# One image's top-k attention and the next stage's state scan: the attention cut into pieces and issued between the scan's steps

## The chip, the cores and the metric

The kernel runs on one core of one Trainium2 chip. The metric is device time in microseconds for one launch, all eight images included. Four compute engines work side by side, each on its own queue and strictly in the order of that queue: TensorE (PE, matmuls, with its weight loads listed as PEld), VectorE (DVE), ScalarE (ACT) and GpSimd (POOL). SyncE (SP) issues the DMAs, in order as well. An instruction whose inputs are not ready holds up everything behind it on its engine. SBUF is the large on-chip memory; PSUM is the small one that TensorE writes, in eight banks of 512 float32 per partition.

## The reference

Input `x` is 8 images of 256 channels by 48 x 48 positions, so 2304 tokens of 256 channels each. Two residual layers follow one another, all in float32.

```python
x = x + _L0_conv_ref(_gn(x), W, bias)        # layer 0: top-16 attention
x = x + _L1_conv_ref(_gn(x), ...)            # layer 1: two Mamba blocks

# layer 0, per image
feat, pos = split(tokens @ W.T + bias)       # 256 channels each
pos = pos / max(norm(pos), 1e-12)
sim = pos @ pos.T                            # 2304 x 2304
topksim, topkid = top_k(sim, 16)
out = softmax(topksim) @ feat[topkid]

# layer 1, per image, twice (DEPTH = 2)
xi, z = split(layernorm(x) @ in_w.T)         # 512 channels each
xc = silu(causal_conv4(xi))
dt, B, C = ... from xc                       # dt: 512, B and C: 16 states
h[t] = h[t-1] * exp(dt[t] * A) + dt[t] * B[t] * xc[t]     # 512 x 16 states
y[t] = sum over states of h[t] * C[t]
x = ((y + xc * D) * silu(z)) @ out_w.T
```

`_gn` is a group normalisation over groups of 8 channels and all positions of an image, so each layer needs the whole image before it starts. The recurrence over the tokens has to run in the order of the tokens.

## The kernel before

The images follow one another. For each, `load_x` (L64) loads the image, `layer0` (L181) computes the attention, and `layer1` (L303) the two Mamba blocks. Each of the two opens its own pools for SBUF and PSUM and closes them at its end (L670 to L675).

`layer0` normalises, projects in six chunks of 384 tokens, and then works through 18 tiles of 128 query tokens (L254). For a tile, PE computes 128 x 2304 similarities in five PSUM pieces, which ACT copies out (L246, L250). DVE finds the 16 largest in four passes over the 2304 columns, two `max` and two `match_replace` (L261 to L264), which mark what was taken; ACT takes the exponential (L268) and DVE masks it (L269). PE transposes the masked row blocks (L275), ACT copies them out (L278), PE multiplies them with the features (L283), and the result is scaled, transposed back and added to the image in SBUF (L285 to L290). The similarities of tile t+1 stand ahead of tile t's selection, and four PSUM buffers for each of two kinds allow that. A scheduler orders this layer.

`layer1` is ordered by hand (`manual_schedule`). Its unit of work is one chunk of 384 tokens at one depth: 12 units per image (`order`, L495). A unit has 16 steps (`STEPS`) of 32 channels; a step holds 32 channels x 4 state groups on 128 partitions, with 4 states (`Q`) in the free dimension, and is done in two parts (`PARTS`) of two states. So a unit is 32 parts and an image 384. The loop over parts `m` (L645) issues for each part, in this order: `carry` (ACT copies the last state column, L565), `decay` of the next part (two ACT exponentials into a PSUM tile `da`, L532), `run_scan` (two DVE scans, L550), and then at even parts POOL's work (`pool_part`, L580; `make_bx` two steps ahead, L518) and DVE's `gate` (L605), at odd parts `sum_states` (PE adds the states up, L595) and `out_proj` (L616).

The scan's result has to be multiplied by C. Which engine does it is set by `on_pool` (L510): in 3 of every 8 parts the scan writes `g` in SBUF and POOL multiplies (L580); in the other 5 the scan writes over `da` in PSUM and DVE multiplies (L556). `g` has four buffers (`LAG` + 2), so the scan of step n needs the state sums of step n-4 done.

What the next unit needs (layer norm, input projection, convolution, B, C, dt and the gates z) is computed by the generator `before` (L341 on) in thirteen pieces, one per part, during the current unit (L665). Its `step_size` part applies softplus and sends `dt` and `dt*x` to HBM through two SBUF buffers each (L469, L473); `load_rep` (L317) reads them back spread over the partitions. PSUM in layer 1: two `da` tiles of two banks, three `mm` banks, one bank `y`.

## Time and profile before

| | |
|---|---|
| median of 3 runs | 14379.09 us (14372.37 to 14391.17) |
| the profiled execution | 14374.63 us |
| its span on the core | 14372.7 us |
| busy, DVE | 10997.1 us (77%) |
| busy, PE | 9414.7 us (66%) |
| busy, POOL | 7832.2 us (54%) |
| busy, ACT | 6977.4 us (49%) |
| first scan instruction of the first image | at 501.7 us |
| first scan instruction of the last image | at 13061.8 us |

Seven images lie between the last two rows, so an image takes 1794.3 us, and the last image's layer 1 takes 1310.9 us to the end. The page's second part shows the busy share of each engine in 40 slices of the span; one image is five of them. The page's fifth part groups instructions by line, engine and shape, with busy time, mean duration, and the idle time before them. The trace can be asked for any stretch of time: the busy time of each engine there, who waited for whom, or the instructions in order. PE durations are modelled; the distance from start to start is the firmer number.

### The profile page before, as it was taken

The page shows a single profiled execution, that of the slowest core. Times are in us where ns is not written, and L with a number is a line of the kernel's source. Part 1 is how long each engine was busy: PE and PEld are TensorE (multiplying, and loading weights), DVE is VectorE, ACT ScalarE, POOL GpSimd, SP SyncE. Part 2 cuts the span into 40 slices and gives each one's busy share as a digit, 9 for nine tenths or more (in the row PEclk, how much of TensorE's full clock was granted, in tenths as well). Part 3 has the DMA queues.
Part 4 walks back from the last instruction along what each step waited for, and adds up shares of the span by engine and source line. Part 5 has one row for each costly group of instructions (what it writes and reads, how often), then busy time and mean ns, then how long its engine had stood idle before and what let it go on. Part 6 is the DMA issues. An engine that isn't in the chain of part 4 may idle for free.

```text
span 14372.7 us, 111023 instructions
## 1 busy us (share of the span) xinstructions
PE 9414.7 (66%) x34144; PEld 4778.3 (33%) x34144; DVE 10997.1 (77%) x12021; ACT 6977.4 (49%) x12922; POOL 7832.2 (54%) x4060
## 2 busy tenths in 40 slices
PE   8656596555965559655596555966559655596655
PEld 6322263222632226322263222632226322263222
DVE  6688866888668886688866888668886688866888
ACT  3455534555345553455534555345543455434554
POOL 0477704777047770477705777057770577705777
PEclk9777797777977779777797777977779777797777
DMA  0233302333023330233302333033330333302333
GB/s 19 67 90 85 88 3 67 88 88 87 3 70 87 87 85 3 70 88 87 84 3 71 87 87 84 3 71 87 87 84 3 72 86 88 84 3 71 86 89 79
DMA packets 634854, 960.01 MB, mean 67 GB/s; under 512 B 88560, under 2 KB 608880, under 8 KB 634256
## 3 DMA queue, kind: packets, MB, share of 16 engines
q1 hardware_dynamic: 621312, 948.75, 27.9%
q8 instruction: 269, 4.41, 0.1%
q10 hardware_dynamic: 12944, 4.16, 0.1%
q14 instruction: 329, 2.70, 0.1%
HBM read 778.01 MB, written 174.59 MB: 66 GB/s over the span
## 4 chain that ended last, share of the span: by engine, by line
DVE 36%; PE 31%; ACT 16%; DMA 9%; issue 4%; SPq 2%; POOL 2%; DVEq 0%; ACTq 0%; POOLq 0%
DVE da L550 18%; ACT da L532 9%; DVE g L556 8%; PE po L283 7%; PE psim L246 7%; DVE g L550 4%; DMA dt_d<-dt 4%; DVE xc L409 4%; PE px L436 3%; PE pe L335 2%; PE pt L275 2%; DMA BC<-bc_d 2%; PE y L595 2%; DMA dtxr<-dtx_d 2%; PE pw L616 1%
## 5 line engine op out<-in xcount | busy, mean ns | idle before, releaser
L518 POOL TENSOR_TENSOR bx<-BC,dtxr 128x1536 f32<-128x1536 f32 x1536 | 5270.5, 3437 | 613.2 <-DVE da L550 531.7
L532 ACT ACTIVATE da<-dtr,A_sb 128x384 f32<-128x384 f32 x6144 | 3578.0, 584 | 1389.7 <-DVE g L550 711.1
L550 DVE TENSOR_TENSOR_SCAN da<-da,h_st,bx 128x384 f32<-128x384 f32 x3200 | 3255.6, 1017 | 1174.8 <-ACT da L532 759.7
L595 PE MATMUL y<-g,sel 128*32 128x384 f32 x12288 | 2651.0, 596 | 572.9 <-DVE g L556 542.0
L580 POOL TENSOR_TENSOR g<-g,BC 128x768 f32<-128x768 f32 x1152 | 2083.1, 1808 | 312.8 <-DVE g L550 231.1
L556 DVE TENSOR_TENSOR g<-da,BC 128x768 f32<-128x768 f32 x1920 | 1838.9, 958 | 141.9 <-DVE da L550 2.8
L382 POOL MEMSET vn<- 128x6 f32 x16 | 1.7, 106 | 3416.1 <-PE pr L288 3416.1
L550 DVE TENSOR_TENSOR_SCAN g<-da,h_st,bx 128x384 f32<-128x384 f32 x1920 | 1839.8, 1000 | 0.0
L335 PE MATMUL pe<-vn,in_sb 128*128 128x384 f32 (+1 forms) x3072 | 1251.8, 550 | 536.6 <-ACT z L488 299.2
L595 PEld LDWEIGHTS y<-g,sel 128*32 128x32 f32 x12288 | 743.9, 130 | 2463.8 <-issue 1595.5
L565 ACT COPY h_st<-da 128x2 f32<-128x2 f32 x1600 | 256.4, 160 | 2233.0 <-DVE g L556 2229.9
L589 PE MATMUL y<-xc,dmat 128*128 128x384 f32 x768 | 452.6, 681 | 1295.4 <-DVE yz L605 1295.4
L616 PE MATMUL pw<-yz,ow_sb 128*128 128x384 f32 x1536 | 732.3, 635 | 845.0 <-DVE yz L605 845.0
L246 PE MATMUL psim<-pos 128*128 128x512 f32 (+1 forms) x2880 | 1155.2, 550 | 0.0
L283 PE MATMUL po<-feat,aT 128*128 128x256 f32 x5184 | 1143.9, 379 | 0.0
L436 PE MATMUL px<-xc,xp_sb 128*48 128x384 f32 x768 | 458.8, 771 | 869.3 <-ACT xc L430 869.3
L283 PEld LDWEIGHTS po<-feat,aT 128*128 128x128 f32 x5184 | 974.3, 190 | 128.2 <-ACT aT L278 1.7
L550 DVE TENSOR_TENSOR_SCAN da<-da,bx 128x384 f32<-128x384 f32 x640 | 613.1, 958 | 520.1 <-ACT da L532 261.8
L335 PEld LDWEIGHTS pe<-vn,in_sb 128*128 128x128 f32 x3072 | 594.3, 206 | 1185.1 <-ACT z L488 357.8
L474 POOL TENSOR_TENSOR dtx<-dt,xc 128x384 f32<-128x384 f32 x384 | 374.6, 994 | 970.5 <-ACT dt L470 969.8
L579 POOL COPY h_st<-g 128x2 f32<-128x2 f32 x960 | 180.1, 188 | 1212.8 <-DVE g L550 1205.3
L409 DVE SCALAR_TENSOR_TENSOR xc<-pe,cw,xc 128x384 f32<-128x384 f32 x1152 | 705.8, 614 | 88.0 <-ACT xc L402 48.0
(124 smaller groups left out, 10595.4 us busy)
## 6 DMA issues: line engine op xcount, KB each, us to landing
dtr<-dt_d SPq DMA_DIRECT2D x1536, 192.0 KB, 3.7
dtxr<-dtx_d SPq DMA_DIRECT2D x1536, 192.0 KB, 5.5
BC<-bc_d SPq DMA_DIRECT2D x768, 192.0 KB, 4.8
dt_d<-dt SPq DMA_DIRECT2D x384, 192.0 KB, 4.3
dtx_d<-dtx SPq DMA_DIRECT2D x384, 192.0 KB, 4.2
x<-in_x_dram SPq DMA_DIRECT2D x48, 384.0 KB, 3.8
out_dram<-x SPq DMA_DIRECT2D x96, 192.0 KB, 1.9
bc_d<-dbl SPq DMA_DIRECT2D x96, 48.0 KB, 1.5
```

Of the source, the lines that this page charges most:

```text
L246: nc.tensor.matmul(pm, pos[:, k, t * P : (t + 1) * P], pos[:, k, c0 : c0 + w], start=(k == 0), stop=(k == CB - 1),)
L283: nc.tensor.matmul(po, aT[:, m, :], feat[:, m, :], start=(m == 0), stop=(m == NB - 1))
L335: nc.tensor.matmul(pe, in_sb[:, d, k, e * P : (e + 1) * P], unit["vn"][:, k, lo:], start=(k == 0), stop=(k == CB - 1),)
L409: nc.vector.scalar_tensor_tensor(xc[e], unit["pe"][e][:, k : k + T], cw[:, d, e, k : k + 1], xc[e], ALU.mult, ALU.add,)
L436: nc.tensor.matmul(px[0:E, :], xp_sb[:, d, k, :], xc[k], start=(k == 0), stop=(k == DB - 1))
L518: nc.gpsimd.tensor_tensor(bx, unit["BC"][0], unit["dtxr"][k][:, i % J : i % J + 1, :].to_broadcast([P, Q, T]), ALU.mult,)
L532: nc.scalar.activation(da[:, q], unit["dtr"][k][:, i % J, :], AF.Exp, scale=A_sb[:, unit["d"], i, s : s + 1],)
L550: nc.vector.tensor_tensor_scan(h[:, q], da[:, q], unit["bx"][i][:, s], 0.0 if unit["c"] == 0 else h_st[:, unit["d"], i, s : s + 1], ALU.mu ...
L556: nc.vector.tensor_tensor(g, h, unit["BC"][1][:, p * HQ : (p + 1) * HQ], ALU.mult)
L580: nc.gpsimd.tensor_tensor(g, g, unit["BC"][1][:, qs], ALU.mult)
L595: nc.tensor.matmul(unit["y"][k][o : o + G, :], sel, unit["g"][ii][:, q], start=False, stop=True, skip_group_check=True,)
L616: nc.tensor.matmul(pw, ow_sb[:, unit["d"], k, cb * P : (cb + 1) * P], unit["ys"][k], start=(k == 0), stop=(k == DB - 1),)
```

## The change

All images become one pipeline. `layer0` is now a generator that is stopped after each piece, and the loop over the parts of the scan takes one piece of the next image's attention per part (`next(other, None)`). Only the first image's attention runs by itself, by draining the same generator. The parts of all images form one list of units, so the preparation (`before`) of an image's first unit runs inside the last unit of the image ahead.

For a tile of 128 queries the generator stops 16 times: five pieces for the selection (two `max`, two `match_replace`, and the mask, with the end of the previous tile's work in the first three), then eleven for the transposes, the products with the features and the next tile's similarities. The first selection piece of a tile always falls on part 15 or 31 of a unit. The whole attention of an image takes 339 of the 384 parts: 47 ahead of the first tile (statistics, projections, first similarities), 284 for the tiles, 8 to close.

To make room: the attention has one PSUM bank `mm0` and one `po`, the scan's side one bank `mm` (three before) beside `da` and `y`; the image is not kept in SBUF but read twice from HBM for layer 0 and once more for its residual, and the result of layer 0 goes to HBM (`x1`) and comes back chunk by chunk; the input and output projection weights are loaded once per unit; `bx` has two buffers (three before) and is made one step ahead (two before); dt and dt*x come back in pieces of two steps (four before); the similarities have one buffer.

Other edits: `on_pool` gives POOL 5 of 8 parts for all images but the last, and where both parts of a step are POOL's it multiplies them in one instruction; `dt` has four buffers; the gates z are computed in a generator of their own (`gates`, from part 7 of the same unit on, its silu at part 11); `before` starts at part 11; square root and reciprocal become exponential of a logarithm on ACT and a Newton step of three small DVE instructions; the image's normalisation moves from DVE to ACT; the second normalisation's statistics are taken in 18 x 2 pieces of 128 columns.

```diff
-    xpool = ctx.enter_context(tc.tile_pool(name="xpool", bufs=NCH))
+    keep = ctx.enter_context(tc.tile_pool(name="keep", bufs=2))
+    ps = ctx.enter_context(tc.tile_pool(name="ps", bufs=2, space=PSUM))
+    ctx.enter_context(tc.manual_schedule())
+    def mm(w, name):
+        return ps.tile([P, 512], F32, tag="mm", name=name, bufs=1)[:, :w]
+    def mm0(w, name):
+        return ps.tile([P, 512], F32, tag="mm0", name=name, bufs=1)[:, :w]
...
+    def rsqrt_end(r, var, eps, name):
+        t = small.tile(list(r.shape), F32, tag="newton", name=f"nt_{name}")
+        nc.vector.scalar_tensor_tensor(t, r, -0.5, r, ALU.mult, ALU.mult)
+        nc.vector.scalar_tensor_tensor(t, var, eps, t, ALU.add, ALU.mult)
+        nc.vector.scalar_tensor_tensor(r, t, 1.5, r, ALU.add, ALU.mult)
...
         def similarity(t):
-            s = rows.tile([P, N], F32, tag="sim", name=f"sim_{b}_{t}")
+            s = keep.tile([P, N], F32, tag="sim", name=f"sim_{b}_{t}", bufs=1)
+            pm = None
             for c0 in range(0, N, SW):
                 w = min(SW, N - c0)
-                pm = psum(w, "mm", f"psim_{b}_{t}_{c0}")
+                if pm is not None:
+                    nc.scalar.copy(s[:, c0 - SW : c0], pm)
+                pm = mm0(w, f"psim_{b}_{t}_{c0}")
...
-                nc.scalar.copy(s[:, c0 : c0 + w], pm)
-            return s
+                yield s
+            nc.scalar.copy(s[:, c0:], pm)
+            yield s
+
+        def attend(t, r):
+            po = ps.tile([P, 512], F32, tag="po", name=f"po_{b}_{t}", bufs=1)[:, :C]
+            pt, aT = None, None
+            for m0 in range(0, NB + 8, 4):
+                if aT is not None:
...
+                        nc.tensor.matmul(
+                            po, aT[1][:, m - aT[0], :], feat[:, m, :],
+                            start=(m == 0), stop=(m == NB - 1),
+                        )
...
+                    nc.scalar.copy(
+                        aT[1][:, 0:n, :], pt[1].rearrange("p (m q) -> p m q", q=P)
+                    )
...
+                        nc.tensor.transpose(
...
+                yield po
...
+            nc.vector.max(top[:, 0:8], s)
+            next(done, None)
+            yield
+            nc.vector.match_replace(r, top[:, 0:8], s, TAKEN)
+            next(done, None)
+            yield
+            nc.vector.max(top[:, 8:16], r)
+            next(done, None)
+            yield
...
+            nc.scalar.activation(s, s, AF.Exp)
+            nc.vector.match_replace(r, top[:, 8:16], r, TAKEN)
+            yield
+            nc.scalar.activation(top, top, AF.Exp, accum_out=den)
+            nc.vector.reciprocal(den, den)
+            nc.vector.scalar_tensor_tensor(r, r, TAKEN, s, ALU.is_equal, ALU.mult)
+            yield
+            ahead = similarity(t + 1) if t + 1 < NB else iter(())
+            for i, po in enumerate(attend(t, r)):
+                if i * 4 >= NB:
+                    s = next(ahead, None)
+                yield
+            for s in ahead:
+                yield
+            done = finish(t, po, den)
...
-                dt = tmp.tile([P, T], F32, tag="dt", name=f"dt_{u}_{k}", bufs=2)
+            dt = keep.tile([P, T], F32, tag="dt", name=f"dt_{u}_{k}", bufs=4)
             nc.scalar.activation(dt, pds[k], AF.Softplus, bias=dtb[:, d, k : k + 1])
-                if k == 0:
-                    step_size(3)
+            if k + 1 < DB:
+                step_size(k + 1)
...
+    def gates(unit):
+        u = unit["u"]
+        in_proj(unit, DB)
+        yield
+        for e in range(DB):
+            z = keep.tile([P, T], F32, tag="z", name=f"z_{u}_{e}", bufs=4)
+            nc.scalar.copy(z, unit["pe"][DB + e])
+            unit["z"].append(z)
+            if e + 1 < DB:
+                in_proj(unit, DB + e + 1)
+                yield
+        nc.scalar.preload_act_table_set("silu_and_others")
+        for e in range(DB):
+            nc.scalar.activation(unit["z"][e], unit["z"][e], AF.Silu)
+        nc.scalar.preload_act_table_set("natural_log_exp_and_others")
...
-        def on_pool(i, p):
-            return p == PARTS - 1 and i % J < J - 1
+    def on_pool(unit, i, p):
+        if unit["b"] + 1 < B:
+            return p == PARTS - 1 or i % J == 0
+        return p == PARTS - 1 and i % J < J - 1
...
-            bx = keep.tile([P, Q, T], F32, tag="bx", name=f"bx_{b}_{n}", bufs=3)
+        bx = keep.tile([P, Q, T], F32, tag="bx", name=f"bx_{n}")
...
+    for _ in layer0(0, lefts[0]):
+        pass
+    load_v(units[0])
+    for _ in before(units[0]):
+        pass
...
+    for m in range(PARTS * (NSTEP + LAG + 4)):
...
+        if m % (HOOKS * len(order)) == 0:
+            image = m // (HOOKS * len(order)) + 1
+            other = layer0(image, lefts[image]) if image < B else iter(())
+        carry(m - 1)
+        decay(m + 1)
+        run_scan(m)
+        if p == 0:
+            make_bx(n + 1)
+            pool_part(n - 1)
+            gate(n - LAG - 1)
+            load_out(n - LAG)
+        else:
+            sum_states(n - LAG)
...
+        next(leaving, None)
+        if unit is not None:
...
+            if m % HOOKS == PARTS * (LAG + 1) + 1:
+                behind = gates(unit)
+            next(behind, None)
+            if follow is not None and m % HOOKS == FRONT:
...
+                load_v(follow)
+                front = before(follow)
+            next(front, None)
+        next(other, None)
-    for b in range(B):
-        xs = load_x(b)
-        with ExitStack() as stack:
-            layer0(b, xs, stack)
-        with ExitStack() as stack:
-            layer1(b, xs, stack)
```

More of the change, by code (lines that the diff above doesn't have):

```diff
@@ new lines, in tile_conv_preact, with at @@
+    order = [
+        (i - d, d) for i in range(NCH + DEPTH - 1) for d in range(DEPTH) if 0 <= i - d < NCH
+    ]
+    lefts = [{} for _ in range(B)]
+    units = [
+        dict(b=b, c=c, d=d, u=f"{b}_{c}_{d}", left=lefts[b], pe={}, xc=[], BC=[], z=[], pw=[],
+             dt_d=[], dtx_d=[], dtr={}, dtxr={}, bx={}, g={}, da={}, y={})
+        for b in range(B) for c, d in order
+    ]
+    following = {(un["b"], un["c"], un["d"]): un for un in units}
+    NSTEP = len(units) * STEPS
+    def at(n):
+        return units[n // STEPS], n % STEPS, n % STEPS // J
@@ new lines, in carry, with pool_part @@
+    def carry(m):
+        n, p = divmod(m, PARTS)
+        if not 0 <= n < NSTEP:
+            return
+        unit, i, k = at(n)
+        if unit["c"] + 1 < NCH and not on_pool(unit, i, p):
+            nc.scalar.copy(
+                h_st[:, unit["d"], i, p * HQ : (p + 1) * HQ], unit["da"][i, p][:, :, T - 1]
+            )
+    def pool_part(n):
+        if not 0 <= n < NSTEP:
+            return
+        unit, i, k = at(n)
+        lo = [p for p in range(PARTS) if on_pool(unit, i, p)]
+        if not lo:
+            return
+        qs = slice(lo[0] * HQ, (lo[-1] + 1) * HQ)
+        g = unit["g"][i][:, qs]
+        if unit["c"] + 1 < NCH:
+            nc.gpsimd.tensor_copy(h_st[:, unit["d"], i, qs], g[:, :, T - 1])
+        nc.gpsimd.tensor_tensor(g, g, unit["BC"][1][:, qs], ALU.mult)
```

774 lines of the change are left out of this document (369 added, 405 removed).

## The prediction

> **What bounds the kernel now.** First the page's slices: an image is five of them, and its first has a lower DVE share, an idle POOL and PE at nine tenths of its clock; the other four are the scan.
>
> ```profile
> DVE  6688866888668886688866888668886688866888
> POOL 0477704777047770477705777057770577705777
> ...
> PEclk9777797777977779777797777977779777797777
> ```
>
> Next the busy times (PE, PEld, DVE, ACT, POOL, then granted clock, DMA share, GB/s) in three stretches of the second image: attention, the head of layer 1 before the first scan, the scan.
>
> ```profile
> 1828.00:2243.00 415.00, 387.59 (x1604) 279.04 (x1604) 274.34 (x250) 152.15 (x265) 0.10 (x1) 0.94 0.00 1
> 2243.00:2297.00 54.00, 30.44 (x72) 15.47 (x72) 9.46 (x16) 25.74 (x38) 7.01 (x5) 0.69 0.44 108
> 2297.00:3620.00 1323.00, 763.06 (x2592) 304.27 (x2592) 1089.25 (x1233) 694.26 (x1313) 971.81 (x501) 0.75 0.36 86
> ```
>
> Three bounds in turn: in the attention PE (388 of 415 us) with POOL idle (0.10), in the head a chain, in the scan DVE (1089 of 1323). Attention's DVE work, 274, is what might move under the scan. Who stopped DVE in the scan stretch, and what held ACT (us, times, longest):
>
> ```profile
> DVE da L550 <- ACT da L532: 123.2, 26, 13.1
> DVE da L550 <- issue: 47.8, 6, 12.1
> DVE da L550 <- POOL bx L518: 29.5, 1, 29.5
> ```
>
> ```profile
> ACT dt L470 <- DMA dt_d<-dt: 94.5, 21, 9.8
> ```
>
> Over 200 of the 234 idle us are waits for da, bx or issue; behind them stands ACT, held 94.5 us by the store of dt from its two buffers. Last, the instructions in order, in a steady piece of scan and in one attention tile, and POOL's and ACT's groups:
>
> ```profile
> 2714.35 2.08 DVE L550 TENSOR_TENSOR_SCAN da<-da,h_st,bx 128x384 f32<-128x384 f32 x2
> ...
> 2716.46 0.96 DVE L556 TENSOR_TENSOR g<-da,BC 128x768 f32<-128x768 f32 x1
> ...
> 2717.33 2.08 DVE L550 TENSOR_TENSOR_SCAN da<-da,h_st,bx 128x384 f32<-128x384 f32 x2
> ...
> 2720.39 1.92 DVE L550 TENSOR_TENSOR_SCAN g<-da,h_st,bx 128x384 f32<-128x384 f32 x2
> ...
> 2722.22 2.06 DVE L550 TENSOR_TENSOR_SCAN da<-da,h_st,bx 128x384 f32<-128x384 f32 x2
> ```
>
> ```profile
> 2066.71 2.13 PE L275 MATMUL pt<-ident,left 128*128 128x128 f32 x18
> ...
> 2067.31 2.56 DVE L261 MAX8 top<-sim 128x8 f32<-128x2304 f32 x1 [4.02 <-ACT sim L250]
> ...
> 2068.67 7.94 PE L283 MATMUL po<-feat,aT 128*128 128x256 f32 x36
> ...
> 2078.23 2.54 DVE L269 SCALAR_TENSOR_TENSOR left<-left,sim 128x2304 f32<-128x2304 f32 x1
> ...
> 2078.50 6.18 PE L246 MATMUL psim<-pos 128*128 128x512 f32 x16
> ...
> 2085.12 2.56 DVE L261 MAX8 top<-sim 128x8 f32<-128x2304 f32 x1 [3.42 <-ACT sim L250]
> ```
>
> ```profile
> L518 POOL TENSOR_TENSOR bx<-BC,dtxr 128x1536 f32<-128x1536 f32 x1536 | 5270.5, 3437 | 613.2 <-DVE da L550 531.7
> L532 ACT ACTIVATE da<-dtr,A_sb 128x384 f32<-128x384 f32 x6144 | 3578.0, 584 | 1389.7 <-DVE g L550 711.1
> ...
> L580 POOL TENSOR_TENSOR g<-g,BC 128x768 f32<-128x768 f32 x1152 | 2083.1, 1808 | 312.8 <-DVE g L550 231.1
> ```
>
> A part multiplied by DVE costs it 2.98 us (2714.35 to 2717.33), one left to POOL 1.83 (2720.39 to 2722.22). A tile goes from max to max in 17.81 us; PE's 18 transposes take 2.13, 36 products 7.94, the similarities 1.77 per 512 columns (three and a half such pieces in 6.18), 8.0 in all: 18.5 with 0.44 of closing transposes. Each of DVE's five passes takes 2.54 to 2.56.
>
> **The cut of the time.** Before: 501.7 to the first scan, 7 x 1794.3, 1310.9 for the last image, 14372.7. After, the same cut: E + 7P + Z. The profiled execution is 14374.63, 1.9 over its span; the median lies 4.5 above it.
>
> **E, the exposed first attention.** Statistics end near 32 as now (constants). Projection: a chunk takes 11.6 now (six in 76 us) with four PSUM buffers; with one bank each matmul group waits for the copy ahead; adding up one chunk's matmuls, copies and small steps in series gives 15, six 90. First similarities 11. A tile: DVE's own 14.7 (2 x 2.59 + 2 x 2.66 + 2.7 for mask and reciprocal, 1.5 closing); then PE's 18.2 and, since one bank serves transposes and similarities, about 3.5 of copies left uncovered: 36.5 against 17.8. Eighteen are 657, closing 10: 800. Head 54 now, 62 with one mm bank: **E = 862**, 360 later than now.
>
> **Z, the last image.** Parts stay 5:3, 20.4 us per 8, with 0.46 of gate 20.9: 83.4 per unit; convolutions (12 of 0.61) and norms add 9.8. The dt wait (94.5/12 = 7.9 per unit) goes with four buffers. Late next: ACT at part 11, where the gates' silu with two table loads (1.28 each) stands ahead of the next unit's norm, whose result DVE's next instruction waits for (about 7), and the softplus block, four times 0.58 with a matmul between each and two table loads, about 8.5 against 4.8 of DVE parts in hand (7 with silu). 12 x 107 = **1290** with the tail.
>
> **P, one merged image.** A unit's 32 parts are 20 of POOL's (1.83) and 12 of DVE's (2.98). Per unit DVE has 74 for parts and gates, 9.8 as above, two tiles at 14.7: 113, plus small steps 115. POOL has 16 bx of 3.44, the multiplies at 1.81 and 3.44 with state copies of 0.19, 4 dtx of 1: 98, so moving two parts in eight there costs nothing while DVE's passes cover it. They do in the selection pieces alone. So four stretches:
>
> - Parts 31 to 3, selection: DVE 4 x 1.83 + 2.98 + 14.7 = 25; all else is shorter. Take 26.
> - Parts 4 to 14, transposes, products, similarities, plus output projection, gates z and the next norm: PE 18.5 + 5.3 + 5.3 (16 records each; a 512-column record takes 0.44, so 0.33 for 384) + 5.9 (32 records of state sums at 0.16, pairs in different columns, and the D term) + 4.1 (the norm's three groups, 6.1 in the head at clock 0.69) = 39. DVE has 30, POOL 32. The output projection, first in PE's queue, needs the last gate (3.5). With one bank each, an ACT copy waits for PE and the next matmul for that copy; the state sums stand behind these matmuls, and until they are done `g` is not free and the scan of part 8 waits. At part 11 ACT's z copy, silu with tables and the norm's scaling (0.5 + 4.3 + 1.3, say 6) stand ahead of the mean that DVE waits for, with the scans of parts 12 on behind it. 3.5 + 39 + 6 = 48.5; DVE idles 18.
> - Parts 15 to 19, selection with convolutions: 25 + 7.7 = 33; take 33.5.
> - Parts 20 to 30, with silu, x_proj, softplus: POOL 32 + 4 = 36, PE 30 (18.5 + 5.3 + 5.9), DVE 27; the softplus block holds ACT, and with it the decays and scans, 6 beyond that: 42.
>
> 150 per unit. The 284 tile parts are 8.9 units: 1331. The 47 parts ahead: 11 at POOL's 3.0, 21 with projections at 4.2 (DVE 71, ACT stalls 17), 15 at 4.1 with PE ahead: 183. Eight closing parts at 3.6: 29. The 44 without attention, POOL-bound at 2.95 plus ACT stalls: 152. **P = 1695**, 99 under now.
>
> Costed at nothing: the extra DMA (x three times more, x1 out and back, weights per unit, 33 MB on 120 per image), hidden under a DMA share of 0.36; wholly uncovered it would be 330 us per image at 100 GB/s. SP issues 64 pieces of dt and dt*x per unit (32 before) and some 30 others, at 0.45 about 42 us of 141. C's load waits for a buffer until the unit's last bx, parts 23 to 29, with the queue behind it; the attention's own transfers fall on parts 15 to 17 and 31 to 1, clear of it. Also bx with two buffers: made 3.44 after its part begins, needed two parts later.
>
> **Unknowns.** PE's clock: 0.94 in attention, 0.75 in the scan; I take the former, because PE works almost without gaps in the long stretch. At 0.75 PE's 39 becomes 49: 164 per unit, with the projections P = 1838. On the good side each stretch takes only its busiest engine, 26 + 39 + 33 + 36 = 134: P = 1553. DVE and POOL side by side: the mask (two SBUF operands) and the Newton steps run beside POOL for the first time; before, POOL was busy 0.10 us there. The nearest rows, scans with one SBUF operand beside POOL, are not stretched (1.02 against 0.96 to 1.0): 0, which I take. Upper end one POOL multiply of 3.44 at each of 18 masks and 20 Newton places, 131 per image.
>
> The Trainium skill, SBUF — State Buffer, section Who interferes with whom, speaks against the change there: a VectorE instruction with two SBUF inputs and a GpSimd instruction that reads SBUF take turns whole. No row of before can show it. By it about 36 per image would be added, mostly Newton steps that meet a bx just started, and the sum would be 14,270 in place of 14,020.
>
> **Sum.** 862 + 7 x 1695 + 1290 = 14,017; with 1.9 around the span and the median 4.5 above it, 14,025.
>
> **Rivals.**
> 1. Forecast (P 1630 to 1740), 0.37.
> 2. PE's share is colder than I take, P = 1838: 862 + 12,866 + 1290 = 15,018. For it: PE waits for ACT copies in every piece, as in the scan stretch, where its clock is 0.75. Against: 39 us of work in 48. It decides from P = 1746, 51 above mine, 5.7 us per unit. Slower, 0.22.
> 3. VectorE and POOL take turns in all places: P = 1826, 14,934. Against: POOL has emptied its queue when the mask runs. 0.10.
> 4. Each stretch takes its busiest engine only, P = 1553: 13,023. For: in the scan now, DVE waits almost only where ACT is held, and buffers smooth a part or two. Against: single PSUM banks. 0.22.
> 5. Everything hides under DVE, P = 1385 (115 per unit): 11,847. Against: PE and DVE peak in different parts and `g` lets PE lag four steps only. 0.06.
> 6. The change does not overlap: single banks expose all of a tile's 21.8 after selection beside 1290 of scan, P near 1900: 15,450. 0.03.
>
> A measurement tells 0.2%, 29 us, from no change. Slower: 2, 3 and 6, 0.35, of which 0.01 goes to no change: 0.34; cases 1, 4 and 5 give 0.65, of which 0.02 goes there: 0.63; same 0.03. The range reaches to 4's end and nearly to 3's: 13,000 to 14,900; the forecast alone spans 13,560 to 14,330.
>
> **What would show it.** First scan near 862 (wrong: below 800, single banks cost less). Period between images 1695. In a unit, DVE idle in parts 4 to 14, released by PE sums and the mean, and at the softplus block; none in selection. ACT's wait for the dt store gone. Granted clock near 0.9 in merged images. Mask rows at 2.54: no taking turns; longer, or Newton steps with idle before them: rival 3. The forecast is wrong if parts 4 to 14 take much other than 48 us.

## The result

The changed kernel takes 14768.57 us (median of 4 runs, 14765.03 to 14774.0) where the kernel before, on the same chip, takes 14384.3 (4 runs): ratio 1.0268, 95% interval 1.0251 to 1.0286. It is 2.7% slower; the forecast was 14,025, faster. The time stays inside the stated range of 13,000 to 14,900, on the wrong side of the kernel before. Cut at the first scan of the first image and of the last (the profiled executions):

| us | to the first scan (E) | one merged image (P, mean of 7) | last image (Z) |
|---|---|---|---|
| before | 501.7 | 1794.3 | 1310.9 |
| forecast | 862 | 1695 | 1290 |
| after | 933.9 | 1777.4 | 1394.9 |

The first attention lies bare and is 432 longer, the last image 84 longer, and each image between gains only 17, so 7 x 17 = 119 stands against 516. The forecast was short in all three: by 72, 7 x 82 = 576 and 105.

Profile after. The slices of the page (DVE, POOL and granted clock):

```profile
DVE  2347777677776777767777777767777677777888
POOL 0026666666676666766667666666666666677667
PEclk7778887788777878778877887878788788877777
```

The five-slice rhythm is gone: nearly every slice has about 0.7 of DVE and 0.6 of POOL, and PE is no longer at 0.9 of its clock a fifth of the time. But nothing is full either. The stretches: projections and tiles of the first attention, head of layer 1, then in merged images the parts ahead of the tiles (243 us), one unit with tiles (150), one without (127), and a unit of the last image (117). A unit is 32 tile parts. Columns: PE, PEld, DVE, ACT, POOL, granted clock, DMA share, GB/s.

```profile
40.00:173.00 133.00, 100.32 (x244) 57.44 (x242) 16.70 (x48) 22.24 (x43) 0.00 (x0) 0.65 0.05 13
173.00:870.00 697.00, 389.85 (x1349) 254.56 (x1348) 253.01 (x218) 139.27 (x230) 0.00 (x0) 0.76 0.03 7
870.00:934.00 64.00, 28.29 (x60) 13.10 (x60) 11.11 (x26) 19.38 (x32) 7.56 (x6) 0.61 0.33 91
2710.00:2953.00 243.00, 176.19 (x590) 89.93 (x590) 163.77 (x211) 112.91 (x217) 140.16 (x76) 0.77 0.28 81
3182.00:3332.00 150.00, 105.00 (x374) 53.29 (x374) 113.61 (x122) 73.14 (x135) 100.34 (x52) 0.82 0.29 83
4361.00:4488.00 127.00, 72.52 (x223) 27.76 (x222) 88.71 (x102) 59.66 (x100) 97.30 (x40) 0.73 0.36 106
13950.00:14067.00 117.00, 67.56 (x222) 25.95 (x222) 95.32 (x108) 60.82 (x118) 81.47 (x44) 0.74 0.34 100
```

The unit with tiles took what was forecast, 150. The parts ahead of the tiles took 243 for 183 and the unit of the last image 117 for 107. The forecast's 152 for 44 parts without attention makes 111 per unit; this one took 127 (123 from its first scan to the next unit's). In the 127 no engine works more than 97 of them. What DVE waited for over the whole run (us, times, longest):

```profile
DVE g L628 <- PE y L674: 1372.1, 167, 13.7
...
DVE v L445 <- PE lm L444: 406.9, 48, 10.3
DVE bt L445 <- PE lm L444: 353.9, 48, 9.3
DVE n L271 <- PE pn L265: 312.7, 48, 16.8
...
DVE pos L282 <- PE pb L198: 122.0, 48, 6.9
```

`g` waits for the sums of the step four back, `v` and `bt` for the mean of the layer norm, `n` and `pos` for the norm of attention's positions. All of these are waits for PE; the largest that is not, 435.7 for ACT's copies of the similarities (`top`), falls on the 18 tiles of the first image's bare attention. PE itself is busy only 67% of the span; its own largest waits are for DVE (1155 for the mask `left`, 956 for the convolution `xc`). ACT's wait for the store of dt, 94.5 per image before, is no longer among its waits, as forecast.

One more row has no counterpart before, the last Newton instruction of the layer norm, three numbers per partition (ns: min/median/max):

```profile
L164 DVE SCALAR_TENSOR_TENSOR rs<-nt_rs,rs x96: 161/3161/3222, 883.0 to 14597.5; 128x3 f32<-128x3 f32 x96
```

### The profile page after: what moved, and what is told of

It reads as the page before. It is cut to its first block, busy times and chain, and to the rows that moved or that the text cites. A ratio compares the mean times of both kernels' runs of the same rounds, so it can differ in the third digit from the quotient of the medians.

```text
span 14770.2 us, 117757 instructions
## 1 busy us (share of the span) xinstructions
PE 9848.7 (67%) x34144; PEld 4871.0 (33%) x34144; DVE 10770.4 (73%) x11869; ACT 7017.9 (48%) x12866; POOL 9317.2 (63%) x4676
## 4 chain that ended last, share of the span: by engine, by line
DVE 44%; PE 28%; ACT 9%; issue 8%; POOL 7%; DMA 2%; SPq 2%; ACTq 0%; DVEq 0%; POOLq 0%
DVE da L628 10%; DVE g L628 9%; PE po L317 5%; PE y L674 5%; DVE g L634 4%; DVE xc L490 4%; PE pe L423 4%; POOL bx L596 4%; ACT da L610 4%; DVE left L381 3%; PE pd L517 3%; PE psim L302 3%; PE pw L703 2%; DVE left L377 2%; DVE left L369 2%
## 5 line engine op out<-in xcount | busy, mean ns | idle before, releaser
L628 DVE TENSOR_TENSOR_SCAN g<-da,h_st,bx 128x384 f32<-128x384 f32 x3040 | 2898.6, 999 | 1231.9 <-PE y L674 1226.4
L659 POOL TENSOR_TENSOR g<-g,BC 128x1536 f32<-128x1536 f32 (+1 forms) x1488 | 3256.8, 2189 | 99.3
L628 DVE TENSOR_TENSOR_SCAN da<-da,h_st,bx 128x384 f32<-128x384 f32 x2080 | 2119.6, 1019 | 341.2 <-issue 117.5
L423 PE MATMUL pe<-vn,inw 128*128 128x384 f32 (+1 forms) x3072 | 1501.8, 621 | 1049.6 <-DVE xc L490 955.7
L634 DVE TENSOR_TENSOR g<-da,BC 128x768 f32<-128x768 f32 x1248 | 1195.4, 958 | 164.9 <-PE y L674 93.2
L336 PE MATMUL pt<-ident,left 128*128 128x128 f32 x2592 | 518.0, 330 | 1174.6 <-DVE left L381 1154.8
L423 PEld LDWEIGHTS pe<-vn,inw 128*128 128x128 f32 x3072 | 636.8, 227 | 1737.8 <-ACT da L610 1204.2
L703 PE MATMUL pw<-z,ow 128*128 128x384 f32 x1536 | 739.6, 636 | 373.5 <-DVE xr L712 181.4
L517 PE MATMUL pd<-dbl,dtp_sb 16*128 16x384 f32 x768 | 605.5, 887 | 551.4 <-ACT dbl L510 299.9
L328 ACT COPY aT<-pt 128x512 f32<-128x512 f32 (+1 forms) x720 | 389.5, 541 | 914.0 <-PE pt L336 913.3
```

Of the source, the lines that this page charges most:

```text
L423: nc.tensor.matmul(pe, unit["inw"][:, k, e % DB * P : (e % DB + 1) * P], unit["vn"][:, k, lo:], start=(k == 0), stop=(k == CB - 1),)
L517: nc.tensor.matmul(pd, dtp_sb[:, d, k * P : (k + 1) * P], dbl[0:R, :], start=True, stop=True)
L628: nc.vector.tensor_tensor_scan(h[:, q], da[:, q], unit["bx"][i][:, s], 0.0 if unit["c"] == 0 else h_st[:, unit["d"], i, s : s + 1], ALU.mu ...
L634: nc.vector.tensor_tensor(g, h, unit["BC"][1][:, p * HQ : (p + 1) * HQ], ALU.mult)
L659: nc.gpsimd.tensor_tensor(g, g, unit["BC"][1][:, qs], ALU.mult)
L703: nc.tensor.matmul(pw, unit["ow"][:, k, cb * P : (cb + 1) * P], unit["z"][k], start=(k == 0), stop=(k == DB - 1),)
```

## The experiments

Every kernel is compared with 14,769 for the changed kernel, which did not run again, and about 14,385 for the one before, which ran beside each. Lengths of units and parts are read from the starts of the scans in the order of instructions.

### The lock: no Newton step

```diff
         rsqrt_start(rs, pv, eps5)
-        rsqrt_end(rs, pv, 1e-5, f"rs_{u}")
```

> One edit to the changed kernel: the layer norm of a unit leaves out the Newton step behind its reciprocal root (three VectorE instructions on 128x3, which the kernel before left out too; the root is then the Ln and Exp alone). In the profiled changed kernel the last of the three lasts 3.1 us at the median where the same form elsewhere lasts 0.16, 96 of them, 301 us together, while POOL multiplies for bx. Theory A (the time is VectorE's own, for a resource that POOL holds, and VectorE is on the path there): 301 us and the two shorter instructions go, 14,430 to 14,490. Rival B (the time passes to the next instruction on VectorE, which meets the same POOL work): 14,690 to 14,770, not more than the short instructions themselves, 48 x 0.5 to 1.5 us.

Measured: 14427.48, 341 less, 3 beyond theory A's range; P 1732.7 (45 less), Z 1362.8 (32 less), E the same within 1.4. The time does not pass on to the next instruction, so theory A holds. "The lock" is a short name for VectorE and GpSimd taking turns. (With 12 units per image the steps are 96, where the expectation counts 48.) The order of instructions of the changed kernel shows why, first DVE's, then POOL's (start, duration):

```profile
2362.86 0.16 DVE L163 SCALAR_TENSOR_TENSOR nt_rs<-lv,nt_rs 128x3 f32<-128x3 f32 x1
2363.06 3.21 DVE L164 SCALAR_TENSOR_TENSOR rs<-nt_rs,rs 128x3 f32<-128x3 f32 x1
2366.20 2.07 DVE L628 TENSOR_TENSOR_SCAN da<-da,h_st,bx 128x384 f32<-128x384 f32 x2
```

```profile
2362.84 3.42 POOL L596 TENSOR_TENSOR bx<-BC,dtxr 128x1536 f32<-128x1536 f32 x1 [10.09 <-issue]
```

The second of the three, which has one of its inputs in PSUM (`lv`), began 0.02 after `bx` and takes 0.16. The third, with both in SBUF, starts 0.22 after `bx` and lasts 3.21, to 2366.27; `bx` ends at 2366.26. It is recorded as work, not as a wait, so no list of waits shows it. It is no single case: 95 of the 96 are long, and each of these ends within 0.06 us of an instruction on POOL, while the second instruction never lasted more than 163 ns. 301 us lie in this one row. The mask, whose two inputs are in SBUF as well, has 3241 ns at the mean for 2541 before, another 101. One that began while a `bx` ran, DVE and then POOL:

```profile
3123.65 4.14 DVE L381 SCALAR_TENSOR_TENSOR left<-left,sim 128x2304 f32<-128x2304 f32 x1
```

```profile
3121.93 3.45 POOL L596 TENSOR_TENSOR bx<-BC,dtxr 128x1536 f32<-128x1536 f32 x1 [6.96 <-DVE g L628]
3125.33 2.51 POOL L658 COPY h_st<-g 128x2 f32<-128x2 f32 x1
```

The mask takes its 2.4 after the end of `bx`, and POOL's small copy, 0.18 elsewhere, lasts until the mask ends. Where the mask begins first it keeps its 2.54, and the `bx` begun 0.11 after it lasts 5.73 for 3.44. The Trainium skill, SBUF — State Buffer, section Who interferes with whom, which the prediction weighed and set aside, says that VectorE instructions with two SBUF inputs and GpSimd instructions that read SBUF take turns whole. This trace agrees, at 3.2 us a time in the Newton row.

### Part 11: the preparation starts one part later

```diff
-    FRONT = 11
+    FRONT = 12
```

> One edit: the work that goes ahead of a unit's scan (layer norm, projection, convolution, step sizes) starts one tile part later, at part 12 of the unit before instead of part 11, so that the mean's matrix product is not queued on TensorE and on the single bank behind the last piece of the gates, whose silu and two table loads on ScalarE stand in part 11. Theory A (the 12.1 us part is a collision of the two on one bank: VectorE waits 407 us in all for the mean's product over 48 units): about 5 us per unit less, 14,480 to 14,600. Rival B (the wait is that product's own chain, copies of v on ScalarE included, and only moves one part on): 14,740 to 14,800.

Measured: 14550.78, 218 less; P 1751.4, Z 1350.8. Theory A holds. In the changed kernel the order at part 11, DVE and then PE:

```profile
2345.27 1.92 DVE L628 TENSOR_TENSOR_SCAN g<-da,h_st,bx 128x384 f32<-128x384 f32 x2
2356.47 0.95 DVE L445 TENSOR_TENSOR bt<-bt,lm 128x768 f32<-128x768 f32 x1 [9.28 <-PE lm L444]
```

```profile
2348.20 1.45 PE L423 MATMUL pe<-vn,inw 128*128 128x384 f32 x4
2349.49 1.02 PE L317 MATMUL po<-feat,aT 128*128 128x256 f32 x4
2350.36 1.88 PE L302 MATMUL psim<-pos 128*128 128x512 f32 x4
2352.17 2.77 PE L674 MATMUL y<-g,sel 128*32 128x384 f32 x16
2354.87 1.56 PE L444 MATMUL lm<-bt,ones_mean 128*128 128x384 f32 x4
```

The mean's product `lm` stands last on PE, behind the product for the last gate, attention's products and similarities and sixteen sums, which PE works off almost without a gap from 2348.20 on. DVE's next instruction needs it and waits 9.28, with the next scan behind it. One part later it has, in the kernel with the edit:

```profile
DVE g L628 <- PE y L674: 925.7, 235, 7.0
DVE g L628 <- ACT da L610: 549.3, 161, 6.7
...
DVE v L445 <- PE lm L444: 157.6, 48, 5.6
...
DVE bt L445 <- PE lm L444: 99.1, 35, 5.6
```

761 us of waits for `lm` became 257 and 1372 for the sums 926, but 549 for decays (2 before the edit) and 302 for DVE's product with the sums (93) took up part of it. With the other start the Newton row also fell to 1509 ns on average, 156 us in all; how much of the 218 came from there is not shown, and the two savings add nearly in full further down.

### The softplus block in two halves

```diff
                 unit[f"{what}_d"].append(sd)
+            if k == 1:
+                nc.scalar.preload_act_table_set("natural_log_exp_and_others")
+                yield
+                nc.scalar.preload_act_table_set("softplus")
```

> One edit: the four softplus of a unit with their products and stores stand in two parts, two in each, with the table switched back to exp between them. In the changed kernel all four stand in one part, which lasts 14.9 us where its neighbours last 2 to 3: ScalarE makes no decay for the next scans as long. Theory A (the pile is the cost, and each half finds cover in scans already made ready): 5 to 8 us per unit less, 14,380 to 14,530. Rival B (the chain of product, softplus, product over one bank is as long either way, and two more table loads of about 1.3 us come on top): 14,770 to 14,900.

Measured: 14810.05, 41 more, as rival B has it: in a unit with tiles the part of some 15 us became one of 12.1 to 12.9 and one of 4.4, and the two together last 16.5 to 17.3, where that part and its neighbour lasted 16.7 to 17.0. The 96 x 2 x 1.28 of table loads on ACT on top were mostly hidden. That the chain of products through one bank sets the length fits this, but no run took it apart.

### What attention adds to a merged image, and the banks

```diff
-    lefts = [{} for _ in range(B)]
+    lefts = [{}] * B
...
-            other = layer0(image, lefts[image]) if image < B else iter(())
+            other = iter(())
```

> Leaves out the attention of images 1 to 7: every image scans the attention result of the first one. All else stands as in the changed kernel. It measures what attention adds to a merged image. Theory A (a unit without tile work lasts 127 us in the merged image, as the 44 parts without attention show): 7 x 12 x 127 = 10,668, with the first image's 934 and the last one's 1395: 12,997, and the attention of an image costs 253 of its 1777. Rival B (units lie nearer to those of the last image, 117.5, as only the POOL share differs): 7 x 12 x 117.5 + 2329 = 12,199, and attention costs 367 per image. Rival C (VectorE's work for attention, some 480 us per image, is all added): 1777 - 480 = 1297 per image, 11,400.

Measured: 12333.36; P 1429.5. Rival B's bound is the nearer (units of 119). So attention adds 1777.4 - 1429.5 = 348 to a merged image; before, an image's attention and head took 1794 less the 1323 of its scan, 471. By this cut the pipeline hides 123 of 471. But layer 1, which took 1323, takes 1430 even with nothing beside it: 107 are lost again. 123 less 107 is, up to rounding, the 17 that an image gained. Which of the edits made for the pipeline costs the 107?

The next kernel goes on from this one. `mm0` and `po` stand idle in it, and the units' products go round three banks, as many as the kernel before gave them:

```diff
+    free = {"banks": 1, "k": 0}
...
-        return ps.tile([P, 512], F32, tag="mm", name=name, bufs=1)[:, :w]
+        tag = ("mm", "mm0", "po")[free["k"] % free["banks"]]
+        free["k"] += 1
+        return ps.tile([P, 512], F32, tag=tag, name=name, bufs=1)[:, :w]
...
+            free["banks"] = 3
             other = iter(())
```

> The changed kernel with the attention of images 1 to 7 left out (12,333 by itself; every image scans the attention result of the first), and the units' matrix products go round the three banks mm, mm0 and po, of which the last two stand idle then: as many as the kernel before had for them. Theory A (the units last 119 us and not 111 because each product waits until the one bank has been read): units of about 112 and a last image of about 1330, 12,333 less 84 x 7 less 65: 11,650 to 11,800. Rival B (the lock of the Newton step, GpSimd's larger share and the start at part 11 make the 8 us, and the bank costs nothing beside VectorE and GpSimd): 12,230 to 12,340.

Measured: 11503.14, 830 less, a larger saving than theory A's range; P 1326.6, Z 1276.5. 103 of the 107 are back, with the Newton step and the start at part 11 (losses) and the unheld dt (a gain) still in. A unit with one bank and with three:

```profile
1402.00:1523.00 121.00, 72.30 (x222) 27.78 (x222) 86.76 (x98) 61.96 (x115) 96.22 (x53) 0.73 0.33 96
```

```profile
1372.00:1484.00 112.00, 67.42 (x222) 26.96 (x222) 86.56 (x97) 61.37 (x115) 95.74 (x53) 0.76 0.37 103
```

and what PE waited for with one bank:

```profile
PE y L668 <- DVE z L683: 901.6, 98, 11.8
PE pe L423 <- DVE xc L490: 825.5, 288, 4.1
```

The second line is a convolution's product that waits for DVE to read the one before; behind it DVE waits for ACT's first step of the next convolution, 402.8 in all. With three banks:

```profile
PE pe L427 <- DVE xc L494: 39.2, 97, 2.8
```

DVE's 402.8 became 31.4. All products of a unit share these banks, so the 103 is the price of the one bank for all of them; the convolution's share in it was not taken apart, and neither was the price beside a running attention, which needs the other two banks.

### Five g buffers

```diff
-            xr = keep.tile([P, CB, P], F32, tag="xr", name=f"xr_{b}_{t}")
+            xr = keep.tile([P, CB, P], F32, tag="xr", name=f"xr_{b}_{t}", bufs=1)
...
-            unit["g"][i] = keep.tile([P, Q, T], F32, tag="g", name=f"g_{n}", bufs=LAG + 2)
+            unit["g"][i] = keep.tile([P, Q, T], F32, tag="g", name=f"g_{n}", bufs=LAG + 3)
```

> One edit: five buffers for the scans' results g where the changed kernel has four (the space comes from one buffer for the residual tile xr instead of two, which is loaded a whole tile ahead of its next use). VectorE's largest wait in the changed kernel is the scan that writes g, held until TensorE has summed the states out of that buffer four steps before: 1372 us in all. Theory A (the wait is only lack of a buffer: TensorE is late for some parts and catches up): more than half of the 1372 goes, 13,800 to 14,100. Rival B (TensorE stands behind matrix products that wait for ScalarE and the single bank, so that the next thing VectorE needs from it is as late): 14,600 to 14,790, and the waits come up at the mean's product, the gate and the output projection.

Measured: 14705.66, 63 less. Rival B is right in the time, but not in the place where the waits come up. DVE's waits with five buffers:

```profile
DVE g L628 <- ACT da L610: 798.5, 204, 8.9
...
DVE v L445 <- PE lm L444: 411.3, 48, 10.3
...
DVE da L628 <- POOL h_st L658: 336.2, 74, 5.3
DVE da L628 <- issue: 294.5, 119, 5.1
```

The 1372 for the sums are gone from the list, and 798 for decays, 336 for POOL's states and 294 for issue (2, none and 136 with four) stand there. The largest wait of the run was worth a twentieth of its size. ACT's own wait for the convolution's products is as large as it was (1108 us, 1116 with four buffers), so it may be that ACT is late for the same products; no run shows it.

### GpSimd's share

```diff
-        if unit["b"] + 1 < B:
-            return p == PARTS - 1 or i % J == 0
```

> One edit to the changed kernel: GpSimd takes the product with C for 3 of 8 tile parts in every image (as it does in the last one), not for 5 of 8 in the first seven. Per unit 8 products of 0.96 us go to VectorE and 8 halves of one of 2.2 us leave GpSimd. Theory A (VectorE is what a merged unit lasts by, and gets the 7.7 us): 84 x 7.7 = 647 more, about 15,400. Rival B (the units wait on TensorE's sums, on GpSimd's bx and its lock, and shorter GpSimd turns give back what VectorE adds): 14,600 to 14,900.

Measured: 15077.37, 309 more, between the two; P 1821.7, 44 more where DVE's added work is 92 per image. About half of it found cover. Of the two shares, the larger for POOL is the better one in this pipeline.

### The norm spread out, and where the tiles meet the unit

This kernel starts the preparation at part 12 as well.

```diff
+            yield
 
             n2 = small.tile([P, TB], F32, tag="n2", name=f"n2_{b}_{c}")
             nc.vector.tensor_scalar(n2, pn, 1e-24, None, ALU.max)
             pf = features(0)
+            rn = small.tile([P, TB], F32, tag="rn", name=f"rn_{b}_{c}")
+            rsqrt_start(rn, n2, 0.0)
             yield
             keep_features(0, pf)
             pf = features(1)
-            rn = small.tile([P, TB], F32, tag="rn", name=f"rn_{b}_{c}")
-            rsqrt_start(rn, n2, 0.0)
...
             pb = spread(rn, TB, mm0, f"pb_{b}_{c}")
+            yield
```

> Two edits: the start at part 12 (14,551 by itself), and in attention's projections the norm of the positions is spread over more tile parts: a part between the sum of squares on TensorE and VectorE's read of it, one between the reciprocal root's spread on TensorE and VectorE's product with it, and the root's Ln and Exp one part ahead of its Newton step. So no VectorE instruction stands in the part of the product that it needs; there are 12 more parts per image in which attention is at work. Theory A (the 47 parts ahead last 243 us and not 183 because VectorE waits there in the same part for TensorE: 298 us in all for the norm's sum, 110 for the spread): 300 to 400 less than with the start at part 12 alone, 14,150 to 14,250. Rival B (these parts are long by the units' own waits, which stay, and the wait only moves to the scan): 14,480 to 14,560.

Measured: 14758.12, 207 more than the start at part 12 alone, a miss for both theories. DVE's wait for the norm fell from 298 to 66, and the first two units of the first image became 135.5 and 139.5 from 157 and 151 (144.7 and 140.0 from 164.7 and 147.8 in most others). But most units with tiles became 153.6 or 157 in place of 146.8 or 150. Either the spread norm slows them, or the 12 parts by which the tiles now start later. Two kernels tell these apart by idle parts ahead of each attention: four (`for _ in range(4): yield`) with the spread norm, twelve without.

> The start at part 12 and the spread norm, as in the run before, and four idle tile parts ahead of every attention, so that the 18 tiles start 16 parts later than with the start at part 12 alone, not 12. A tile takes 15.8 parts and a unit 32, so two tiles meet the same parts of every unit: by 16 parts later the meeting is what it was, by 12 it is another. Theory A (the spread norm does shorten the parts ahead of the tiles, 308 to 275 us over the first two units, and 12 parts of shift made the nine units with tiles 155.4 instead of 148.5 us long): the units with tiles are back at 147 to 151, an image lasts about 1751 less 33, all 14,543 less 230: 14,280 to 14,360. Rival B (the spread norm itself slows the units, by its parts or by ScalarE's order): units with tiles of 153 to 157, 14,700 to 14,780.

> The start at part 12, the norm as in the changed kernel, and 12 idle tile parts ahead of every attention: the shift of the spread norm without the spread norm. Theory A (which part of a unit a tile's instructions meet is worth 60 us per image): units with tiles of 153 to 157, an image of about 1800, 14,850 to 14,970. Rival B (the meeting is worth nothing): 14,530 to 14,570.

Measured: 14448.7 and 14981.8. Four parts more take 309 us off; twelve idle parts alone add 431. Most units with tiles are 146.8 and 150.2 in the first and 153.6 and 157.1 in the second, the lengths of the kernels with the same shift. So where a tile's work meets a unit is what counts, 6.8 us per unit. The spread norm itself is worth 32 per image at a shift of 12 (1815.1 to 1782.9), and 14 at one of 16 against none (1751.4 to 1737.6), so that the first kernel stays 89 above theory A's range; why 14 and not 32 is open. A tile takes 16 parts, half a unit, so a shift by 16 leaves the meeting as it was and a shift by 12 does not. Next to each other, a unit with tiles with the start at part 12 alone and one shifted by 12:

```profile
1539.00:1686.00 147.00, 100.78 (x374) 50.73 (x374) 114.66 (x123) 75.91 (x140) 100.98 (x53) 0.85 0.28 82
```

```profile
1550.00:1707.00 157.00, 109.00 (x374) 56.14 (x374) 113.83 (x122) 75.65 (x140) 100.77 (x53) 0.76 0.27 79
```

The instructions are the same, 374 on PE; DVE is as busy. PE takes 109.0 for 100.8, at a clock of 0.76 for 0.85. DVE's waits over the run grow where ACT is late, 830 for 549 at the decays and 300 for 70 at the convolution. The lock does not explain it: the Newton row is smaller in the shifted kernel (50 us for 145), the mask's larger by 61. Whether PE's clock is colder because the unit is longer, or the unit longer because of the clock, these runs do not tell apart.

### All together

Without the Newton step, start at part 12, five `g` buffers, the spread norm, and the first image's attention round three banks (`mm0`, `mm`, `y`):

> All together: without the layer norm's Newton step, the start at part 12, five g buffers, the projections' norm spread over more parts, and the first image's attention going round the banks mm0, mm and y, two of which stand idle until the first scan. Theory A (the waits lie apart and their savings add): 14,769 less 341, less 218, less what five buffers and the spread norm give by themselves in this call, less 70 to 110 in the 934 us ahead of the first scan: 13,400 to 13,800 if these two do as their first theories say. Rival B (they share the same waits on TensorE): 14,000 to 14,150, still below the kernel before.

Measured: 14397.47, ratio 1.0013 (1.0005 to 1.0022), a miss for both theories: the shift by 12 was in it. E is 795.2, 139 less, more than the 70 to 110 expected. Without the spread norm, and then with it and the four idle parts:

> Without the layer norm's Newton step, the start at part 12, five g buffers, the first image's attention over three banks; the norm of the positions as in the changed kernel. Theory A (the savings add: 49 ahead of the first scan's end by the lock, 26 and 9 per image, 138 before the first scan): 13,980 to 14,100. Rival B (with the start at part 12 the lock has lost half of its 301 us already, so that it gives 20 per image and not 45): 14,120 to 14,250. Both are below the kernel before.

> As the one before, with the spread norm and the four idle parts that keep the tiles where they were in a unit. Theory A (another 33 per image): 13,750 to 14,000. Rival B (with five buffers and without the Newton step the units have another pattern, and 16 parts of shift or the spread norm cost what they save): 14,000 to 14,250.

Measured: 14034.61 (0.9758) and 13906.78 (0.9667). The savings of the Newton step, the start, the fifth buffer and the banks add nearly in full: 341 + 218 + 63 + 139 = 761 by themselves, 734 together. Then the idle banks, first in the last image:

> The best version so far (13,907), and in the last image, beside which no attention runs, the products go round the three banks mm, mm0 and po. Theory A (the one bank is what is left of the longer last image): 1308 us from its first scan to the end become 1240 to 1270, all 13,840 to 13,880. Rival B (the bank is hidden): 13,895 to 13,915.

Measured: 13838.98 (0.9619), 1 beyond theory A's range; Z 1307.7 became 1244.0. And in the merged images wherever attention leaves them idle:

```diff
-            if image == B:
-                free["banks"] = 3
+            free["banks"] = 1 if image < B else 3
...
-        next(other, None)
+        if next(other, "end") == "end":
+            free["banks"] = 3
```

with `mm0` and `po` in turn for the projections.

> The best version so far (13,839) with two more uses of idle banks inside the merged images: from the end of an image's attention to the next image's start the units' products go round mm, mm0 and po, and attention's projections, during which po stands idle, go round mm0 and po. Theory A (the bank is missed in merged images too): some 30 of the 384 parts have three banks, about one unit of 119 becomes 110, and the 59 parts ahead lose a part of their waits for TensorE, 10 to 25 us per image, 13,660 to 13,770. Rival B (with attention in the image VectorE covers it): 13,820 to 13,850.

Measured: 13775.02, ratio 0.9574 (0.9561 to 0.9587): 4.3% faster than the kernel before, 6.7% than the changed one, 5 above theory A's range and 45 below rival B's; an image is 8.4 shorter, less than the 10 to 25 of theory A. Its slices:

```profile
DVE  3467777777777777777777777777877777778888
PEclk8778888788888888888887888878888788887777
```

| us | E | P | Z |
|---|---|---|---|
| before | 501.7 | 1794.3 | 1310.9 |
| after | 933.9 | 1777.4 | 1394.9 |
| best version | 796.5 | 1677.1 | 1240.5 |

## Why the prediction was wrong

- **The sign** came from P. It was put at 1695, with 1746 as the point from which the change loses; it is 1777. With P as forecast and E and Z as measured the sum is about 14,200, still faster; with only P as measured it is about 14,600. The rival that names that point (a colder PE) ends on the right side, but not by its own mechanism: the units with tiles, which it put at 164, last 150 at a granted clock of 0.82. The granted clock "near 0.9 in merged images" did not come: the rows show 0.73 to 0.82. And the forecast's own sign of being wrong, parts 4 to 14 far from 48, would not have caught it: they took 50.
- **The steps that failed** in P are three: the 0 for VectorE and GpSimd side by side, the 183 for the parts ahead of the tiles, and the nothing put down for the units' own products on one bank. By the starts of the scans an image's parts ahead take 245, its tiles 1324, the closing 41 and the rest 168, where the sum has 183, 1331, 29 and 152.
- **The lock at 0**: 341 us, 45 per merged image and 32 in the last. Without it alone the changed kernel takes 14,427, level with the kernel before to 0.3%. The nearest rows, scans beside POOL, did not stretch, and were taken as the answer; they have one input in SBUF, these instructions two. The estimate by the page, 36 per image, was nearer: the run gives 45 for the layer norm's Newton step alone. Of rival 3, which had turns taken at every mask and Newton place at 131 per image, the mechanism came, and about half of the price: this 45, and by the extra length of the rows 101 over the run at the masks and 92 at attention's own Newton steps.
- **The parts ahead of the tiles**, 183 for 47: 245, the largest single miss of P, 62 of 82. The three terms "11 at POOL's 3.0, 21 with projections at 4.2, 15 at 4.1" measured 45, 130 and 69 for 33, 88 and 62. They added up DVE's work and ACT's stalls. But in these parts DVE's instruction stands in the same part as the product that it reads, and waits for PE and through it for ACT; spread over more parts, an image falls by 14 to 32. Of the 62, leaving out the Newton step gave back 9 and the start at part 12 another 13; the rest is open.
- **Parts without attention**, taken as bound by POOL with ACT stalls: 168 for 152. (There are 45 of them, 384 less 339, not 44, which is some 3 of it.) The sum counted what each engine does and left out that the units' products now wait for the one bank. With attention left out the same 45 parts take 169 with one bank and 152 with three, and a whole image 103 less (1430 to 1327). The prediction put the single bank's price into the stretch with the transposes, where PE was expected to be the bound, and gave the units' own products none.
- **The unit with tiles**, 150 by four stretches, came out: 149.9 and 150.5 in turn by the scans' starts, the stretches of the latter 24.0, 50.5, 32.9 and 43.1 for 26, 48.5, 33.5 and 42. The pile at part 11, 6 in that sum, is there; starting one part later gave 2.3 per unit back (218 us over 96 units). Part of the agreement is luck: without the Newton step the units last 146.5 and 147.1, so some 3.4 of the 150 are the lock, which the sum put at 0, and PE's share was worked out at a clock of 0.94.
- **The last image**: 1290 forecast, 1394.9. The sum "83.4 per unit; convolutions and norms add 9.8" has no term for the bank or the lock. Runs give 32 for the Newton step, 44 for part 11 and 64 (best version) to 124 (all else unchanged, attention left out) for the bank. Together that is more than the 105 missed; where the sum was too large for it is open.
- **E**, 862: 933.9. Projections and statistics to 173.5 where 133 was taken, tiles and closing 697 for 667, the head 64 for 62. A chunk takes 20.6 where its added durations gave 15, and a tile 39.2 for 36.5. With three banks they take 11.5 and 34.6, and E falls by 139. So the one bank's chain was the right term, and it was put too low.
- **Costed at nothing**, and no wait on record speaks against it: the extra DMA, the store of dt, two `bx` buffers (DVE waits 59 for `bx` in the whole run). No DMA is among DVE's large waits. No run took one of them away.

## What to carry to other kernels

Before two stages are merged, price what each loses by sharing: here a merged image hid 123 us of attention, while its second layer alone had become 107 longer, of which 103 came back with the two banks that it had given away. When two loops of fixed step run as one, check whether their periods stand in a simple ratio (here 16 parts and 32), because then each collision comes back in every round, and a shift by some steps is worth as much as a real saving (431 us here). A long wait in a list is not its worth; and a small instruction that lasts longer than its size is a wait that the lists of waits here did not show.

## What the runs showed of the hardware

- A VectorE instruction on 128 x 3 lasted 3.2 us, until the GpSimd instruction beside it ended, where the same form alone lasts 0.16; the masks lasted up to 4.2 for 2.54. The other way round, a GpSimd product begun just after a mask lasted 5.73 for 3.44.
- The same 374 PE instructions of a unit took 100.8 us at a granted clock of 0.85 and 109.0 at 0.76, in kernels that differ by twelve idle parts; without attention, with PE busy 60% of a unit, the clock was 0.73 to 0.76.
- Removing 1372 us of VectorE's waits on one resource was worth 63 us of time.
